# The output product of a graph network: two node blocks in seven block products over halves of columns, the third block plain and last

## The chip, the core and the metric

The kernel runs on one core of one Trainium2 chip. The metric is the device time of one execution in microseconds (us), lower is better. All numbers are 32-bit floats. The engines are TensorE (PE in the profile; PEld is its weight load), VectorE (DVE), ScalarE (ACT), GpSimd (POOL) and SyncE (SP, which here only issues DMA transfers). Each takes its own instructions in order; they wait for each other by semaphores.

## What is computed

The program is an attention layer over a graph of 384 nodes, followed by a relational graph convolution network with two layers. Only the second network is touched. In short:

```python
x = relu(h_text @ w_in + b_in)                     # 384 x 768
for l in range(2):
    h_in = x
    x = rgcn_conv(x, src, dst, edge_type, basis[l], comp[l], root[l], conv_bias[l])
    x = relu(x) + h_in
    x = batchnorm(x, bn_gamma[l], bn_beta[l])      # over the nodes
h_final = x @ w_out + b_out                        # 384x768 by 768x1024
result = residual + layernorm(h_final, ln_gamma, ln_beta)   # over the 1024 columns
```

The product `x @ w_out` and the layer normalisation behind it are the end of the program.

## The kernel before

Features lie on the 128 partitions: after a layer, `XT` is a tile of 128 x 6 x 384, six chunks of 128 features by 384 nodes. Nodes make three blocks of 128. A product accumulates over the six chunks in a PSUM bank of 512 columns. Each matmul of 32-bit floats stands in the trace as two records of PE and two of PEld. Most of the program's products are already made by seven block products instead of eight (Winograd's form): sums of blocks are made beforehand on VectorE, and the products are added up in PSUM banks and on the way out of them.

The order of TensorE, VectorE, ScalarE, GpSimd and SyncE is that of the code (`manual_schedule`); the framework only puts in the waits. So an instruction of VectorE that has to wait holds up everything written after it on VectorE.

The second layer (l = 1) ends as follows. Line numbers are those of the profile.

- The last basis products (L979, L985) make `H_`. The root product (L1019, 72 records) begins the six banks `pr`; inside it `rest()` makes the last block product of the basis stage.
- VectorE makes the sums of the mixed adjacency `At` (T1 to T4, L1082 to L1086) and the first feature sums (L1097).
- `first_of(0)` and the products with `q(1, 0)` follow, and then the loop `for p in range(pairs)` with three passes (products at L1077). A pass makes two chunks of features, o0 = 2p and o1 = 2p + 1, in banks `pa` and `pc`. TensorE's order in a pass is S0·T1 into pc, S1·T2 into pa, S3·q(1,1) into pc, S2·T3 into pa, then the first product of the next pair (into the bank `following`) and h(o1,1)·T4 into pa.
- `take(o, j, ps)` (L1107) adds half a chunk from a bank to `XN` on VectorE. A product that goes on accumulating in a bank waits until the `take` of what was there before has read it: S3·q(1,1) waits for `take(o1, 1, pc)`, S2·T3 for `take(o0, 1, pa)`.
- When a chunk is complete, `rectify` applies ReLU on ScalarE (L1110), `measure` takes the batch statistics (L1042 to L1049), and `normalise_layer` applies them (L1054 to L1058). The last two chunks are XN[4] and XN[5].
- The output product (L1183) reads XN. For each node block t it takes two banks of 512 columns (block 2: one of 512 and two of 256). Block 0 runs over k = 0 to 3 for both banks, and then over k = 4 and 5. VectorE adds the bias (L1187), takes row statistics (L1189), makes mean and deviation (`row_spread`, L156 to L159), applies them (L1194, L1195, L1197), and SP and ACT store the halves.
- The output weights `w_out` come in three parts of two chunks (1 MB each) through SP, in a ring of five buffers `wpool`, which the basis and root weights share.

Storage: `T13` and `T2` (sums of weights) lie in the buffers tagged `hT` and `mask8` of the pool `keep`; `S` (node sums) and `T4` in the pool `cp`. In layer 0 the feature sums borrow two weight buffers of `wpool`, too. `sums` and `rn` are small tiles of the pool `late`, used for the edge counts in layer 0.

Of the kernel before, what the change touches and what calls it, by code (L numbers as in the profile page):

```python
# [10 lines left out]
F32 = mybir.dt.float32  # L11
# [4 lines left out]
ALU = mybir.AluOpType  # L16
# [35 lines left out]
def gnn_kernel(ctx: ExitStack, tc: tile.TileContext, out, x, edges, chunks, cols, rows, small,  # L52
# [36 lines left out]
    def wload(src, shape, name, whole=False):  # L89
        w = wpool.tile([P, *shape], F32, tag="w", name=name)  # L90
        load_rows(w, src, whole)
        return w
# [60 lines left out]
    def row_spread(st):  # L153

        mv = tiny.tile([P, 2], F32, tag="mv", name="mv")
        nc.vector.bn_aggr(mv, st.rearrange("p a b -> p (a b)"))  # L156
        sd = tiny.tile([P, 1], F32, tag="sd", name="sd")
        nc.vector.tensor_scalar(sd, mv[:, 1:2], LN_EPS, None, ALU.add)
        nc.scalar.activation(sd, sd, AF.Sqrt)  # L159
        return mv, sd  # L160
# [190 lines left out]
    taken = []  # L351

    def add_up(r):
        sums[r] = late.tile([P, N], F32, tag="sum", name="sum", bufs=4)
        nc.gpsimd.tensor_tensor(sums[r], A[:, r, 0, :], A[:, r, 1, :], ALU.add)
        nc.gpsimd.tensor_tensor(sums[r], sums[r], A[:, r, 2, :], ALU.add)

    def share(r):

        ps = next_bank("ps_cnt", [i for i in range(8) if i not in taken])  # L360
        nc.tensor.matmul(ps[:, :N], ones, sums[r], start=True, stop=True)
        rn = late.tile([P, N], F32, tag="rn", name="rn", bufs=2)

        nc.scalar.activation(rn, ps[:, :N], AF.Relu, bias=minus)
        nc.scalar.activation(rn, rn, AF.Identity, bias=ones[:, 0:1])
        nc.vector.reciprocal(rn, rn)
        nc.vector.tensor_tensor(A[:, r], A[:, r], rn[:, None, :].to_broadcast([P, NT, N]), ALU.mult)
        if r + 4 < R:
            add_up(r + 4)


    with ExitStack() as inner:
# [261 lines left out]
        soft = soft_stack.enter_context(tc.tile_pool(name="soft", bufs=1, side="right"))  # L634
        At = late.tile([P, B, NT, N], F32, name="At")
        A = late.tile([P, R, NT, N], F32, tag="A", name="A")

        prA = keep.tile([P, KD, N], F32, tag="hT", name="prA")
        prB = soft.tile([P, KD, N], F32, name="prB")
# [266 lines left out]
    with tc.tile_pool(name="conv", bufs=1) as cp:  # L906
# [4 lines left out]
        def block(X, n, i):  # L911

            return X.rearrange("p (c i) n -> p i c n", i=2)[:, i, :, n * P:(n + 1) * P]

        def node_sums(X):
            S = cp.tile([P, 4, 3, P], F32, tag="S", name="S")
            for i, a, b, op in ((0, block(X, 1, 0), block(X, 1, 1), ALU.add), (1, S[:, 0], block(X, 0, 0), ALU.subtract),
                                (2, block(X, 0, 0), block(X, 1, 0), ALU.subtract),
                                (3, block(X, 0, 1), S[:, 1], ALU.subtract)):
                nc.vector.tensor_tensor(S[:, i], a, b, op)  # L920
            return S

        def weight_sums(w):
            T13 = keep.tile([P, 3, 2, HC], F32, tag="hT", name="T13")
            T2 = keep.tile([P, 3, HC], F32, tag="mask8", name="T2")
            for c in range(3):
                nc.vector.tensor_tensor(T13[:, c], w[c][:, :, HC:], w[c][:, 0, :].rearrange("p (o d) -> p o d", o=2),
                                        ALU.subtract)
                nc.vector.tensor_tensor(T2[:, c], w[c][:, 1, HC:], T13[:, c, 0], ALU.subtract)
            return T13[:, :, 0], T2, T13[:, :, 1]  # L930

        def last_sums(w, T2):
            T4 = cp.tile([P, 3, HC], F32, tag="T4", name="T4")
            for c in range(3):
                nc.vector.tensor_tensor(T4[:, c], w[c][:, 1, :HC], T2[:, c], ALU.subtract)
            return T4
# [28 lines left out]
        for l in range(L):  # L965
# [3 lines left out]
            for b in range(B):  # L969
# [6 lines left out]
                def times(ps, x, y, start=False):  # L976

                    for c in range(3):
                        nc.tensor.matmul(ps, x[:, c], y(c), start=start and c == 0, stop=(c == 2),  # L979
                                         skip_group_check=not start)  # L980
# [9 lines left out]
                    go_between(l, b, c)  # L990
                nc.scalar.copy(hs[0][0], pa)  # L991
                nc.vector.tensor_tensor(hs[0][0], hs[0][0], pb, ALU.add)
                times(pc, S[:, 0], lambda c: T[0][:, c], True)
                nc.scalar.copy(hs[2][0], pe)
                nc.scalar.copy(hs[2][1], pf)
                nc.scalar.copy(hs[1][1], pc)
                times(pa, S[:, 1], lambda c: T[1][:, c])
                nc.scalar.copy(hs[0][1], pa)
                times(pc, S[:, 3], lambda c: w[c][:, 1, HC:])
                nc.vector.tensor_tensor(hs[0][1], hs[0][1], pc, ALU.add)  # L1000
                times(pa, S[:, 2], lambda c: T[2][:, c])
                nc.vector.tensor_tensor(hs[1][1], hs[1][1], pa, ALU.add)

                def rest(pa=pa, X=XT, T4=T4, dst=hs[1][0]):
# [12 lines left out]
            for k in range(KC):  # L1017
# [3 lines left out]
                if k == 0:  # L1021
                    rest()
                go_between(l, B, k)
            room2 = keep.tile([P, KD * N], F32, tag="hT", name="room2")
            spaces = [room2[:, 2304:]]
            if l + 1 < L:
                spaces += [v.rearrange("p i k o -> p (i k o)")[:, i * 768:(i + 1) * 768] for v, n in
                           ((cp.tile([P, 4, 3, P], F32, tag="S", name="sums"), 2),
                            (wpool.tile([P, 2, 6, P], F32, tag="w", name="sums"), 2)) for i in range(n)]
                spaces.append(cp.tile([P, 3, HC], F32, tag="T4", name="sums").rearrange("p c d -> p (c d)")[:, :768])  # L1030
                w = load_basis(l + 1, 0)
            else:

                room = late.tile([P, R * NT * N], F32, tag="A", name="room")
                spaces += [room[:, 3 * D + i * 768:3 * D + (i + 1) * 768] for i in range(5)]
                rowsB = room[:, :3 * D].rearrange("p (j d) -> p j d", j=3)
                for j, r in enumerate((R_BOUT, R_LNG, R_LNB)):
                    nc.scalar.dma_start(rowsB[:, j, :], rows[r:r + 1, :].to_broadcast([P, D]))

            def measure(o):  # L1040

# [36 lines left out]
                                     skip_group_check=True)  # L1078

            T1, T2 = [room2[:, i * 1152:(i + 1) * 1152].rearrange("p (c d) -> p c d", c=6) for i in range(2)]  # L1080
            T4 = keep.tile([P, 6, HN], F32, tag="mask8", name="T4")
            nc.vector.tensor_tensor(T1, q(0, 1), q(0, 0), ALU.subtract)  # L1082
            nc.vector.tensor_tensor(T2, q(1, 1), T1, ALU.subtract)
            T3 = q(0, 1)
# [40 lines left out]
            for p in range(pairs):  # L1125
# [34 lines left out]
                take(o1 + 1, 0, following)  # L1160
                ready = measure(rectify(o1))
                pa = following
            XT = XN
            if l + 1 < L:
                S = node_sums(XT)
# [2 lines left out]

        for t in range(NT):
            nc.gpsimd.tensor_tensor(x_sb[:, t, :], x_sb[:, t, :], rowsB[:, 2, :], ALU.add)  # L1170
        w = [wload(w_out[part], (2, D), "w_out") for part in range(3)]
        hf_ = cp.tile([P, NT, D], F32, tag="H", name="hf")
        for t in range(NT):
            hf = hf_[:, t, :]
            last = t == NT - 1
            ps = [next_bank("ps_f") for _ in range(3 if last else 2)]

            parts = [(ps[0], 0, 512), (ps[1][:, :256], 512, 768), (ps[2][:, :256], 768, D)] if last else \
                [(ps[0], 0, 512), (ps[1], 512, D)]
            for ks in ((range(4), range(4, KC)) if t == 0 else (range(KC),)):  # L1180
                for p, c0, c1 in parts:
                    for k in ks:
                        nc.tensor.matmul(p, XT[:, k, t * P:(t + 1) * P], w[k // 2][:, k % 2, c0:c1],  # L1183
                                         start=(k == 0), stop=(k == KC - 1))
            st = tiny.tile([P, 4, 6], F32, tag="st", name="st")
            for p, c0, c1 in parts:
                nc.vector.tensor_tensor(hf[:, c0:c1], p, rowsB[:, 0, c0:c1], ALU.add)  # L1187
                for c in range(c0, c1, 256):
                    nc.vector.bn_stats(st[:, c // 256, :], hf[:, c:c + 256])  # L1189
            mv, sd = row_spread(st)  # L1190

            parts = ((nc.sync, slice(0, 512)), (nc.scalar, slice(512, D)))
            for _, cs in parts:
                nc.vector.scalar_tensor_tensor(hf[:, cs], hf[:, cs], mv[:, 0:1], rowsB[:, 1, cs], ALU.subtract, ALU.mult)  # L1194
            nc.vector.reciprocal(sd, sd)  # L1195
            for queue, cs in parts:
                nc.vector.scalar_tensor_tensor(hf[:, cs], hf[:, cs], sd, x_sb[:, t, cs], ALU.mult, ALU.add)  # L1197
                queue.dma_start(out[t * P:(t + 1) * P, cs], hf[:, cs])


def _by_outputs(w, n):
# [68 lines left out]
```

## Time and profile before

| what | us |
|---|---|
| median of 3 runs | 725.38 (724.61 to 729.79) |
| the profiled execution | 717.47 |
| its span, first to last instruction | 715.7 |
| second layer, TensorE in L1077 | 636.3 to 677.3 |
| output product, TensorE in L1183 | 677.1 to 708.2 |
| from the last matmul to the end | 7.5 |

The page of the profile gives each engine's busy time and the chain of work that ended last. The mean granted clock of TensorE is 0.995 of full speed over the span. Views of the trace give the records in order of time with start and length; "idle before" and an arrow name what ended an engine's wait. Times inside the program are counted from the span's start.

In the stretch from 677.1 to 708.2 us, VectorE is busy for 18.3 us, ScalarE for 1.1. After 708.2 only the normalisation of the third block and the stores of its two halves remain.

### The profile page before, as it was taken

How to read it: one execution, taken by the hardware profiler on the slowest of the kernel's cores; microseconds unless marked ns; L12 is line 12 of the kernel's file. 1: busy time of each engine (PE TensorE's matmuls, PEld its weight loads, DVE VectorE, ACT ScalarE, POOL GpSimd, SP SyncE). 2: the span in 40 equal slices, each digit the busy share in tenths (PEclk: the TensorE clock that was granted, in tenths of full speed). 3: DMA queues.
4: the chain of work that ended last, by engine and by line, in shares of the span. 5: the costliest groups of instructions: out<-in, count | busy, mean ns of one | idle time of the engine just before them, and what ended most of it. 6: DMA issues, size and time to landing. Idle time of an engine off the chain costs nothing.

```text
span 715.7 us, 9149 instructions
## 1 busy us (share of the span) xinstructions
PE 699.9 (98%) x3228; PEld 527.9 (74%) x3228; DVE 512.6 (72%) x1307; ACT 157.6 (22%) x360; POOL 308.1 (43%) x239
## 2 busy tenths in 40 slices
PE   8999999999999999999999999999999999999995
PEld 7759999999997444478985555558975555579943
DVE  5886697868886699787534279798878766507756
ACT  3211111111111577410221124202131111011100
POOL 1366777778687788687786542000000000120000
PEclk9999999999999999999999999999999999999999
DMA  8788787373562622733424994311104322700001
GB/s 303 267 279 264 228 250 212 80 243 67 203 209 43 177 2 1 221 44 45 89 0 103 250 288 153 133 44 45 45 0 133 102 69 94 308 1 1 1 30 59
DMA packets 69180, 91.04 MB, mean 127 GB/s; under 512 B 22940, under 2 KB 50688, under 8 KB 68750
## 3 DMA queue, kind: packets, MB, share of 16 engines
q1 hardware_dynamic: 46830, 78.45, 32.6%
q0 software_dynamic: 21296, 9.60, 10.8%
q10 hardware_dynamic: 1008, 2.41, 0.9%
q8 instruction: 25, 0.41, 0.2%
q14 instruction: 21, 0.17, 0.1%
HBM read 79.27 MB, written 11.16 MB: 126 GB/s over the span
## 4 chain that ended last, share of the span: by engine, by line
PE 87%; DVE 10%; ACT 2%; DMA 1%; issue 0%; DVEq 0%; ACTq 0%
PE ps_g L985 12%; PE ps_g L979 10%; PE ps_k L402 10%; PE ps_c L1077 10%; PE ps_v L402 8%; PE ps_q L420 6%; PE ps_q L402 5%; PE ps_f L1183 4%; DVE At L348 4%; PE ps_y L402 3%; PE ps_c L1019 3%; PE ps_x L402 3%; PE ps_o L707 2%; PE ps_s L662 2%; PE ps_pT L696 2%; PE ps_v L586 2%
## 5 line engine op out<-in xcount | busy, mean ns | idle before, releaser
L283 POOL DMA_INDIRECT atab<-count,at x99 | 166.3, 1679 | 44.2 <-issue 23.5
L278 POOL DMA_INDIRECT mtab<-m_val,at x99 | 103.4, 1045 | 57.6 <-issue 22.9
L1170 POOL TENSOR_TENSOR x_sb<-x_sb,room 128x1024 f32<-128x1024 f32 x3 | 7.0, 2348 | 188.9 <-DMA room<-in_rows 188.9
L348 DVE SCALAR_TENSOR_TENSOR At<-A,small_sb,At 128x1152 f32<-128x1152 f32 x40 | 53.6, 1414 | 0.0
L979 PE MATMUL ps_g<-T,S 128*128 128x384 f32 x144 | 49.1, 486 | 0.0
L985 PE MATMUL ps_g<-w_c,XN 128*128 128x384 f32 x144 | 47.7, 487 | 1.1 <-DVE XN L1107 1.1
L985 PE MATMUL ps_g<-w_c,XT 128*128 128x384 f32 x144 | 47.9, 486 | 0.0
L420 PE MATMUL ps_q<-hT,w_q 128*128 128x384 f32 (+1 forms) x160 | 43.4, 435 | 1.4 <-DVE hT L108 1.4
L985 PEld LDWEIGHTS ps_g<-w_c,XN 128*128 128x128 f32 x144 | 27.3, 190 | 20.2 <-DVE XN L1107 1.4
L979 PEld LDWEIGHTS ps_g<-T,S 128*128 128x128 f32 x144 | 27.3, 190 | 19.2 <-ACT H L991 0.4
L985 PEld LDWEIGHTS ps_g<-w_c,XT 128*128 128x128 f32 x144 | 27.3, 190 | 18.8
L420 PEld LDWEIGHTS ps_q<-hT,w_q 128*128 128x128 f32 x160 | 30.1, 200 | 14.1 <-ACT hT L101 1.7
L1077 PE MATMUL ps_c<-At,H 128*128 128x192 f32 x216 | 36.4, 326 | 0.0
L1077 PEld LDWEIGHTS ps_c<-At,H 128*128 128x128 f32 x216 | 35.4, 190 | 0.5
L402 PE MATMUL ps_k<-T,S 128*128 128x192 f32 x192 | 35.1, 326 | 0.0
L1107 DVE TENSOR_TENSOR XN<-XN,ps_c 128x192 f32<-128x192 f32 x38 | 12.5, 349 | 30.8 <-ACT XN L1063 19.7
L402 PEld LDWEIGHTS ps_k<-T,S 128*128 128x128 f32 x192 | 31.8, 190 | 0.0
L1183 PE MATMUL ps_f<-w_out,XN 128*128 128x512 f32 (+1 forms) x84 | 31.1, 531 | 0.0
L675 DVE CUSTOM_DVE_ANT_0 s<-ps_s,mask 128x384 f32<-128x384 f32 x48 | 24.5, 550 | 5.3 <-PE ps_s L662 5.3
L267 DVE SCALAR_TENSOR_TENSOR same<-cells,own,later 128x128 f32<-128x128 int32 x99 | 28.0, 350 | 0.4
L267 DVE SCALAR_TENSOR_TENSOR same<-keys,key,weigh 128x128 f32<-128x128 int32 x99 | 27.9, 349 | 0.0
L1183 PEld LDWEIGHTS ps_f<-w_out,XN 128*128 128x128 f32 x84 | 15.9, 190 | 14.9 <-issue 14.3
(298 smaller groups left out, 1411.6 us busy)
## 6 DMA issues: line engine op xcount, KB each, us to landing
w_c<-in_basis SPq DMA_DIRECT2D x96, 192.0 KB, 4.1
atab<-zero SPq DMA_DIRECT2D x36, 192.0 KB, 5.2
A<-atab POOLq DMA_DIRECT2D x12, 576.0 KB, 9.0
keys<-keys_d SPq DMA_DIRECT2D x25, 192.0 KB, 5.1
w_c<-in_root SPq DMA_DIRECT2D x6, 768.0 KB, 7.1
w_q<-in_wiq SPq DMA_DIRECT2D x16, 256.0 KB, 6.4
w_k<-in_wk SPq DMA_DIRECT2D x16, 256.0 KB, 5.8
w_k<-in_wik SPq DMA_DIRECT2D x16, 256.0 KB, 3.0
```

Source lines behind the costliest of these rows:

```text
L267: nc.vector.scalar_tensor_tensor(same, row[:, n, :], mine[:, c:c + 1], times, ALU.is_equal, ALU.mult, accum_out=count[:, i, c:c + 1])
L278: nc.gpsimd.indirect_dma_start(mtab[c // PER][:, :], bass.IndirectOffsetOnAxis(at[:, 0, c:c + 1], 0), m_val[:, c:c + 1], None)
L283: nc.gpsimd.indirect_dma_start(atab[0 if i < 11 else i % 2][:, :], bass.IndirectOffsetOnAxis(at[:, 1, c:c + 1], 0), count[:, 1, c:c + 1], ...
L348: nc.vector.scalar_tensor_tensor(At[:, b], A[:, r], w, At[:, b], ALU.mult, ALU.add)
L402: nc.tensor.matmul(ps, a[:, k, :], b[:, k, :], start=start and k == 0, stop=(k == 3), skip_group_check=not start)
L420: nc.tensor.matmul(ps[o][:, c], wt_[:, k, o * P:(o + 1) * P], src[:, k, c], start=(k == 0 and c.start == 0), stop=(k == KD - 1 and c.stop ...
L675: nc.vector.tensor_tensor_reduce(s[j], ps[:, :N], mask8[:, t, :], -scale, 3.0e38, ALU.add, ALU.min, tops[:, j:j + 1])
L979: nc.tensor.matmul(ps, x[:, c], y(c), start=start and c == 0, stop=(c == 2), skip_group_check=not start)
L985: nc.tensor.matmul(ps, block(XT, n, i)[:, c], w[c][:, i, o * HC:(o + 1) * HC], start=(first and c == 0), stop=(c == 2 and (i == 1 or ps is ...
L1019: nc.tensor.matmul(pr[o], w[k // 2][:, k % 2, o * P:(o + 1) * P], XT[:, k, :], start=(k == 0), stop=(k == KC - 1))
L1077: nc.tensor.matmul(ps, x[:, c], y[:, c], start=start and c == 0, stop=stop and c == 5, skip_group_check=True)
L1183: nc.tensor.matmul(p, XT[:, k, t * P:(t + 1) * P], w[k // 2][:, k % 2, c0:c1], start=(k == 0), stop=(k == KC - 1))
```

## The change

The output product of node blocks 0 and 1 is made in seven block products over halves: halves of the features (even and odd chunks), two node blocks, and halves of the 1024 columns. Each of the seven has three matmuls of 512 columns. Block 2 stays plain and is made last. The sums of weights (`out_sums`, twelve subtractions of 128 x 512) are made on VectorE in three places: four before the adjacency sums of the last layer, four at the end of the first pass of the pairs, four at the end of the second. The sums of nodes (`OS`, four of 128 x 384) are made after the last normalisation. `w_end` is the load of the output weights, written ahead of the loop. Storage is put together so that room for these sums is found: `x_all`, `room2`, `mroom` and `sum_room` each take the place of several tiles.

```diff
     def add_up(r):
-        sums[r] = late.tile([P, N], F32, tag="sum", name="sum", bufs=4)
+        sums[r] = sum_room[:, r % 4]
...
-        rn = late.tile([P, N], F32, tag="rn", name="rn", bufs=2)
+        rn = sum_room[:, 4 + r % 2]
...
+        sum_room = late.tile([P, 6, N], F32, name="sum_room")
...
+        x_all = cp.tile([P, 4 * 3 * N], F32, name="x_all")
+        x_room = [x_all[:, i * 3 * N:(i + 1) * 3 * N] for i in range(4)]
+        room2 = keep.tile([P, KD * N], F32, tag="hT", name="room2")
+        mroom = keep.tile([P, 6, HN], F32, tag="mask8", name="mroom")
...
             spaces = [room2[:, 2304:]]
             if l + 1 < L:
-                spaces += [v.rearrange("p i k o -> p (i k o)")[:, i * 768:(i + 1) * 768] for v, n in
-                           ((cp.tile([P, 4, 3, P], F32, tag="S", name="sums"), 2),
-                            (wpool.tile([P, 2, 6, P], F32, tag="w", name="sums"), 2)) for i in range(n)]
-                spaces.append(cp.tile([P, 3, HC], F32, tag="T4", name="sums").rearrange("p c d -> p (c d)")[:, :768])
+                spaces += [x_all[:, i * 768:(i + 1) * 768] for i in range(5)]
                 w = load_basis(l + 1, 0)
             else:
...
+                w_end = [wload(w_out[part], (2, D), "w_out") for part in range(3)]
+                out_T = [v.rearrange("p (c o) -> p c o", c=3) for v in
+                         [x_all[:, i * 1536:(i + 1) * 1536] for i in range(3)]
+                         + [sum_room.rearrange("p r n -> p (r n)")[:, :1536]]]
+                def out_sums(*which):
+                    for i, c in which:
+                        x, y = [(b_end(0, 1), b_end(0, 0)), (b_end(1, 1), lambda c: out_T[0][:, c]),
+                                (b_end(1, 1), b_end(0, 1)), (b_end(1, 0), lambda c: out_T[1][:, c])][i]
+                        nc.vector.tensor_tensor(out_T[i][:, c], x(c), y(c), ALU.subtract)
+                def b_end(i, half):
+                    return lambda c: w_end[c][:, i, half * 512:(half + 1) * 512]
+                out_sums((0, 0), (1, 0), (0, 1), (1, 1))
...
                 ready = measure(rectify(o1))
                 pa = following
+                if l + 1 == L:
+                    out_sums(*(((2, 0), (3, 0), (2, 1), (3, 1)) if p == 0 else ((0, 2), (1, 2), (2, 2), (3, 2))))
...
-        w = [wload(w_out[part], (2, D), "w_out") for part in range(3)]
...
+        for dst, x, y, op in ((OS[0], block(XT, 1, 0), block(XT, 1, 1), ALU.add),
+                              (OS[1], OS[0], block(XT, 0, 0), ALU.subtract),
+                              (OS[2], block(XT, 0, 0), block(XT, 1, 0), ALU.subtract),
+                              (OS[3], block(XT, 0, 1), OS[1], ALU.subtract)):
+            nc.vector.tensor_tensor(dst, x, y, op)
+        def put_out(t, c0, ps, first, done):
+            cs = slice(c0, c0 + ps.shape[1])
+            nc.vector.tensor_tensor(hf_[:, t, cs], ps, rowsB[:, 0, cs] if first else hf_[:, t, cs], ALU.add)
+            for c in range(c0, cs.stop, 256) if done else ():
+                nc.vector.bn_stats(st[t][:, c // 256, :], hf_[:, t, c:c + 256])
...
+        def times(ps, x, y, start=False):
+            for c in range(3):
+                nc.tensor.matmul(ps, x[:, c], y(c), start=start and c == 0, stop=(c == 2), skip_group_check=not start)
...
+        pa, pb, pc, pd = [next_bank("ps_f") for _ in range(4)]
+        times(pa, block(XT, 0, 0), b_end(0, 0), True)
+        put_out(0, 0, pa, True, False)
+        times(pb, block(XT, 0, 1), b_end(1, 0), True)
+        put_out(0, 0, pb, False, True)
+        times(pc, OS[0], summed(0), True)
+        put_out(1, 512, pc, True, False)
+        times(pa, OS[1], summed(1))
+        put_out(0, 512, pa, True, False)
+        times(pc, OS[3], b_end(1, 1))
+        put_out(0, 512, pc, False, True)
+        times(pd, block(XT, 1, 1), summed(3), True)
+        put_out(1, 0, pd, True, False)
+        times(pa, OS[2], summed(2))
+        finish(0)
+        put_out(1, 0, pa, False, True)
+        put_out(1, 512, pa, False, True)
...
+        for p, c0 in parts:
+            for k in range(KC):
+                nc.tensor.matmul(p, XT[:, k, 2 * P:], w_end[k // 2][:, k % 2, c0:c0 + p.shape[1]],
+                                 start=(k == 0), stop=(k == KC - 1))
+        finish(1)
+        for p, c0 in parts:
+            put_out(2, c0, p, True, True)
+        finish(2)
```

`block(X, n, i)` is node block n with the even (i = 0) or odd (i = 1) chunks; `summed(i)` is `out_T[i]`; `finish(t)` is the normalisation and the stores of block t as before (`row_spread`, L1194 to L1198). `node_sums`, `weight_sums` and `last_sums` only get their storage from the new tiles.

More of the change, by code (lines that the diff above doesn't have):

```diff
@@ L913, in block @@
             return X.rearrange("p (c i) n -> p i c n", i=2)[:, i, :, n * P:(n + 1) * P]
+        x_all = cp.tile([P, 4 * 3 * N], F32, name="x_all")
+        x_room = [x_all[:, i * 3 * N:(i + 1) * 3 * N] for i in range(4)]
+        room2 = keep.tile([P, KD * N], F32, tag="hT", name="room2")
+        mroom = keep.tile([P, 6, HN], F32, tag="mask8", name="mroom")
         def node_sums(X):
[L916 to L920, printed above, removed]
+            S = [v.rearrange("p (c n) -> p c n", c=3) for v in
+                 [x_room[0][:, i * N:(i + 1) * N] for i in range(3)] + [x_room[1][:, :N]]]
+            for dst, a, b, op in ((S[0], block(X, 1, 0), block(X, 1, 1), ALU.add), (S[1], S[0], block(X, 0, 0), ALU.subtract),
+                                  (S[2], block(X, 0, 0), block(X, 1, 0), ALU.subtract),
+                                  (S[3], block(X, 0, 1), S[1], ALU.subtract)):
+                nc.vector.tensor_tensor(dst, a, b, op)
             return S
         def weight_sums(w):
-            T13 = keep.tile([P, 3, 2, HC], F32, tag="hT", name="T13")
-            T2 = keep.tile([P, 3, HC], F32, tag="mask8", name="T2")
+            T13 = room2[:, :6 * HC].rearrange("p (c o d) -> p c o d", c=3, o=2)
+            T2 = mroom.rearrange("p c n -> p (c n)").rearrange("p (c d) -> p c d", c=3)
             for c in range(3):
@@ L932, in last_sums @@
         def last_sums(w, T2):
-            T4 = cp.tile([P, 3, HC], F32, tag="T4", name="T4")
+            T4 = x_room[2].rearrange("p (c d) -> p c d", c=3)
             for c in range(3):
@@ L992, in gnn_kernel @@
                 nc.vector.tensor_tensor(hs[0][0], hs[0][0], pb, ALU.add)
-                times(pc, S[:, 0], lambda c: T[0][:, c], True)
+                times(pc, S[0], lambda c: T[0][:, c], True)
                 nc.scalar.copy(hs[2][0], pe)
@@ L996, in gnn_kernel @@
                 nc.scalar.copy(hs[1][1], pc)
-                times(pa, S[:, 1], lambda c: T[1][:, c])
+                times(pa, S[1], lambda c: T[1][:, c])
                 nc.scalar.copy(hs[0][1], pa)
-                times(pc, S[:, 3], lambda c: w[c][:, 1, HC:])
+                times(pc, S[3], lambda c: w[c][:, 1, HC:])
                 nc.vector.tensor_tensor(hs[0][1], hs[0][1], pc, ALU.add)
-                times(pa, S[:, 2], lambda c: T[2][:, c])
+                times(pa, S[2], lambda c: T[2][:, c])
                 nc.vector.tensor_tensor(hs[1][1], hs[1][1], pa, ALU.add)
@@ L1023, in gnn_kernel @@
                 go_between(l, B, k)
-            room2 = keep.tile([P, KD * N], F32, tag="hT", name="room2")
             spaces = [room2[:, 2304:]]
             if l + 1 < L:
-                spaces += [v.rearrange("p i k o -> p (i k o)")[:, i * 768:(i + 1) * 768] for v, n in
-                           ((cp.tile([P, 4, 3, P], F32, tag="S", name="sums"), 2),
-                            (wpool.tile([P, 2, 6, P], F32, tag="w", name="sums"), 2)) for i in range(n)]
-                spaces.append(cp.tile([P, 3, HC], F32, tag="T4", name="sums").rearrange("p c d -> p (c d)")[:, :768])
+                spaces += [x_all[:, i * 768:(i + 1) * 768] for i in range(5)]
                 w = load_basis(l + 1, 0)
@@ L1080, in gnn_kernel @@
             T1, T2 = [room2[:, i * 1152:(i + 1) * 1152].rearrange("p (c d) -> p c d", c=6) for i in range(2)]
-            T4 = keep.tile([P, 6, HN], F32, tag="mask8", name="T4")
+            T4 = mroom
             nc.vector.tensor_tensor(T1, q(0, 1), q(0, 0), ALU.subtract)
@@ L1170, in gnn_kernel, with finish @@
             nc.gpsimd.tensor_tensor(x_sb[:, t, :], x_sb[:, t, :], rowsB[:, 2, :], ALU.add)
-        w = [wload(w_out[part], (2, D), "w_out") for part in range(3)]
         hf_ = cp.tile([P, NT, D], F32, tag="H", name="hf")
-        for t in range(NT):
-            hf = hf_[:, t, :]
[L1175 to L1190, printed above, removed]
+        OS = [mroom.rearrange("p c n -> p (c n)")[:, i * N:(i + 1) * N] for i in range(3)] + [room2[:, :N]]
+        OS = [v.rearrange("p (c n) -> p c n", c=3) for v in OS]
+        for dst, x, y, op in ((OS[0], block(XT, 1, 0), block(XT, 1, 1), ALU.add),
[3 more added lines that the diff above has]
+            nc.vector.tensor_tensor(dst, x, y, op)
+        st = [tiny.tile([P, 4, 6], F32, tag="st", name="st") for _ in range(NT)]
+        def put_out(t, c0, ps, first, done):
[3 more added lines that the diff above has]
+                nc.vector.bn_stats(st[t][:, c // 256, :], hf_[:, t, c:c + 256])
+        def finish(t):
+            hf = hf_[:, t, :]
+            mv, sd = row_spread(st[t])
             parts = ((nc.sync, slice(0, 512)), (nc.scalar, slice(512, D)))
@@ L1198, in gnn_kernel, with summed @@
                 queue.dma_start(out[t * P:(t + 1) * P, cs], hf[:, cs])
+        def times(ps, x, y, start=False):
+            for c in range(3):
+                nc.tensor.matmul(ps, x[:, c], y(c), start=start and c == 0, stop=(c == 2), skip_group_check=not start)
+        def summed(i):
+            return lambda c: out_T[i][:, c]
+        pa, pb, pc, pd = [next_bank("ps_f") for _ in range(4)]
[15 more added lines that the diff above has]
+        put_out(1, 512, pa, False, True)
+        ps = [next_bank("ps_f") for _ in range(3)]
+        parts = [(ps[0], 0), (ps[1][:, :256], 512), (ps[2][:, :256], 768)]
+        for p, c0 in parts:
[6 more added lines that the diff above has]
+        finish(2)
 def _by_outputs(w, n):
```

## The prediction

> **What bounds the kernel now.** I read the busy shares first, then the chain of waits near the end, then the timelines of TensorE and VectorE there, because the change acts only there. The busy line and two rows of the chain (start, length, what):
>
> ```profile
> PE 699.9 (98%) x3228; PEld 527.9 (74%) x3228; DVE 512.6 (72%) x1307; ACT 157.6 (22%) x360; POOL 308.1 (43%) x239
> ...
> 636.34 40.95 PE ps_c L1077 x252
> 677.29 30.94 PE ps_f L1183 x84
> ```
>
> TensorE is the bound: from 636.34 to 708.2 us it does nothing but the products of the second layer (L1077) and the output product (L1183), without a gap; then VectorE finishes the last node block and 7.5 us pass to the end (715.7). Work taken from L1183 is therefore worth its full streaming time, and any wait put into L1077 costs its full length. What the stage consists of, and its weights:
>
> ```profile
> L1183 PE MATMUL ps_f<-w_out,XN x84: 379/592/593, 677.1 to 707.8; 128*128 128x512 f32 x60, 128*128 128x256 f32 x24
> L87 SPq DMA_DIRECT2D w_out<-in_w_out x3: 328/328/328, 608.6 to 620.9; - x3
> DMA to landing us min/median/max: 7.8/7.8/7.8
> ```
>
> Each matmul of the code is two records, so these are 30 of 512 columns and 12 of 256. 60 x 512 + 24 x 256 = 36,864 columns in 31.1 us are 0.844 ns a column, 0.864 us for one matmul of 512 columns. The weights have landed by 620.9 + 7.8 = 628.7. Last, where TensorE and VectorE hand over in the last two of the three passes of the loop over pairs (TensorE, then VectorE):
>
> ```profile
> 659.58 2.12 PE L1077 MATMUL ps_c<-At,room 128*128 128x192 f32 x12
> 661.52 4.07 PE L1077 MATMUL ps_c<-At,H 128*128 128x192 f32 x24
> ...
> 671.27 2.11 PE L1077 MATMUL ps_c<-At,room 128*128 128x192 f32 x12
> ...
> 677.12 31.09 PE L1183 MATMUL ps_f<-w_out,XN 128*128 128x512 f32 x84
> ```
>
> ```profile
> 658.29 0.15 DVE L1048 TENSOR_SCALAR sc<-mvb 128x1 f32<-128x1 f32 x1
> 658.36 0.34 DVE L1107 TENSOR_TENSOR XN<-XN,ps_c 128x192 f32<-128x192 f32 x1
> ...
> 665.89 0.95 DVE L1097 TENSOR_TENSOR H<-H 128x768 f32<-128x768 f32 x1
> 666.76 0.95 DVE L1097 TENSOR_TENSOR room<-H,room 128x768 f32<-128x768 f32 x1
> 667.63 0.61 DVE L1107 TENSOR_TENSOR XN<-XN,ps_c 128x192 f32<-128x192 f32 x2
> 668.63 0.56 DVE L1042 TENSOR_TENSOR XN<-XN 128x384 f32<-128x384 f32 x1 [0.39 <-ACT XN L1110]
> ...
> 670.03 0.15 DVE L1048 TENSOR_SCALAR sc<-mvb 128x1 f32<-128x1 f32 x1
> 670.11 0.34 DVE L1107 TENSOR_TENSOR XN<-XN,ps_c 128x192 f32<-128x192 f32 x1
> ...
> 681.57 0.48 DVE L1058 TENSOR_SCALAR XN<-XN,sc 128x384 f32<-128x384 f32 x1
> 685.91 0.69 DVE L1187 TENSOR_TENSOR hf<-ps_f,room 128x512 f32<-128x512 f32 x1 [3.85 <-PE ps_f L1183]
> ```
>
> The matmuls at 659.58 and 671.27 are the products S3·q(1,1). They add into the bank pc that `take(o1, 1, pc)` must have read; that read is the L1107 at 658.36 (ends 658.70) and at 670.11 (ends 670.45). So the slack is 0.88 and 0.82 us: VectorE is 72% busy on average, but here it is nearly in step with TensorE.
>
> **Removed.** Blocks 0 and 1 took 24 matmuls of 512 columns; seven products of three take 21. Three fewer are 3 x 0.864 = 2.6 us, all on the path.
>
> **Added within the pairs: `out_sums` on VectorE.** After `measure(rectify(o1))` of passes 0 and 1 stand four subtractions of 128x512, and the next `take(o1, 1, pc)` is queued behind them. Width: 768 elements last 0.95 and 384 last 0.56, so 512 last 0.69. Independent ones start 0.08 before the one ahead ends (665.89, 666.76, 667.63: 0.87 apart), so 0.61 apart; pass 1 has a dependent pair (0.72). Pass 0 inserts 4 x 0.61 = 2.45 us, pass 1 0.72 + 3 x 0.61 = 2.56. The Trainium skill, "VectorE: DVE Perf Modes", section Terms, has a flush after every op, the next not issuing until the pipe is empty; by that they would be 4 x 0.69 = 2.76 each, 0.5 more together. The row decides: overlap is seen.
>
> Now step by step. Pass 1: take moves from 658.36 to 660.81, ends 661.15; S3 starts at 661.2 instead of 659.58 and ends at 663.25 (a restart costs 0.1: twelve matmuls after the stall at 495.17 took 2.22 instead of 2.11). S2·T3 waits for `take(o0, 1, pa)`, moved by 2.45 to end at 663.56: TensorE starts it at 663.6, 2.1 late. VectorE keeps its 2.45, since between here and pass 2 its waits are for ScalarE's ReLU (L1042), which follow it. Pass 2: `take` at 670.11 + 2.45 + 2.56 = 675.12, ends 675.46; S3 starts at 675.5 instead of 671.27, with its restart 4.3 us late. Equally: 5.0 inserted, less 0.8 slack, plus handover. From there on TensorE leads, and everything, the last normalised block XN[5] (682.05, now 686.4) included, is 4.3 late.
>
> **Output stage.** It starts at 681.4. Formerly eight matmuls (k 0 to 3) came before any needing XN[4] or XN[5]; now pa wants k 0, 2, 4 and pb wants k 1, 3, 5. XN[4] is in time (677.52 + 4.3 = 681.8, wanted at 683.1). XN[5] is wanted after five matmuls, 681.4 + 4.3 = 685.75, and comes at 686.4: 0.65 of stall, 0.1 of restart. The four node sums follow on VectorE (0.56 each): the first ends at 686.9, wanted at 687.4; OS[1] ends about 687.5, wanted at 690; hidden behind pb and pc. Reuse of pa and pc: their first reads (`put_out`, 0.69) queue behind the node sums and end at about 689.1 and 691.3, wanted at 690.0 and 692.6: no stall.
>
> **The tail.** VectorE gets four more additions from PSUM (0.72 with its start) and those sums, 5 us, over a stage that left it idle for 12.8 of 31.1 us (18.3 busy between 677.1 and 708.2); what matters is the order. After pd's product (697.8 by this count) it must do put_out of pd 0.72, finish(0) 3.4 (689.14 to 692.5 today), two put_outs with statistics 1.47 each, finish(1) 3.4, and block 2's first two parts 1.47 + 0.87: ready at 710.6. TensorE ends at 681.4 + 28.5 + 0.75 = 710.7 (33,792 columns x 0.844 = 28.5). A near tie: I add 0.1; late finishing work would next show here, between 0 and 0.6 (if an operation overlapped as little as by the flush rule). The last 7.5 us, block 2 alone, are unchanged.
>
> **Costed at nothing.** The first four `out_sums` stand before L1082 and wait for the second weight part. Loads were issued from 608.63, the second 0.65 later, so VectorE, ready at 611.8, waits until 616.4 and for `rest()` on TensorE until 616.9; it finishes at 619.2, and the weight sums and first feature sums (5.4 + 3.7 us) at 628.3. They are wanted at 643.98: 15.7 us of cover; without it each us would count. SP: the root loads, then the output weights, then stores, the same order as before; the trace already shows these loads run ahead, so there is no queue to be passed. ACT: the three row loads keep their place. POOL: the three residual additions (624.2 to 631.2) are unchanged; VectorE's shifted sums now end beside them, and should that slow them, the 15.7 us cover it. `sum_room`, `x_all`, `room2` and `mroom` rename storage: the waits of the built program stay alike but for layer 0, where two sums no longer occupy weight buffers and SP's 19.4 us wait for L1097 goes. No TensorE wait of the trace is for a weight of layer 1, so 0 (bounds -0.5 to 0).
>
> **Sum.** -2.6 + 4.3 + 0.75 + 0.1 = +2.6 us: span 715.7 to 718.3, the profiled execution 717.47 to 720.0. The median shown, 725.38, is 7.9 above that execution; I put the same difference on it: 728.0, +0.35%.
>
> **Rivals.** *Cover where I see none*: if the inserted subtractions found room (slack larger than the two rows say), only -2.6 + 0.75 stays: 723.5. For it: VectorE idles 28% overall. Against: both slacks are under 0.9 and the insertions are 2.5. Chance 0.14.
>
> *The clock (the slower side)*: the waits come to about 1.6 and 0.5 us in pass 1 and 2.2 in pass 2. The Trainium skill, "TensorE: Matmul & The Clock Gate", section "Part 1: The HAM clock gate", says an idle window of about 3.4 us halves the clock until a busy window has passed. The row: after the 1.07 us wait at 526.6, matmuls last 486 ns as elsewhere and the granted clock stays 1.00. If each of the two waits tripped it, 3.4 us of work would take 6.8 twice: 2.6 + 6.8 = 9.4, 734.8. It decides from an idle stretch near 3.4 us; mine are below. Chance 0.06.
>
> *The change is not what it says*: the built program has 27 matmuls of 512 columns instead of 30, in the order described; chance 0.02 for something that leaves the time at 725.4. What is left, 0.78, is my sum with its sizes.
>
> **From cases to numbers.** Own range of the sum: restart and overlap move it from +1.5 to +3.7; three runs span 724.61 to 729.79, so a median moves by some 2 us: 725 to 731. The rival with cover widens the range down to 722.5; 731.5 leaves out the clock. About 1% (7.3 us) is what a measurement of this kernel tells from no change. Faster by that: no case gets there (the whole gain is 2.6 us), 0.03 for scatter. Slower: the clock 0.06 and unseen delays 0.04, 0.10. Same: 0.87.
>
> **What would show it.** Right: L1183's successors hold 78 records and about 28.5 us; TensorE waits for VectorE before S3 of pass 1 and pass 2 (about 1.6 and 2 us), and once more (about 0.7) at the sixth matmul of the output stage; the output stage starts near 681.4. Wrong: no such waits (cover); a granted clock under 1.00 after them; a VectorE wait for the output weights that reaches past 640; or an end more than 7.7 us behind the last matmul (the tail).

## The result, and the profile after

The changed kernel takes 732.28 us (median of 20 runs) where the kernel before takes 727.65 beside it; the ratio of the two is 1.0039, 95% interval 1.0015 to 1.0064. The medians take in all runs; the ratio compares the fast ones alone, because some runs fell into a slower state. That is 0.4% slower, 2.8 us of 727.65 (between 1.1 and 4.7): a small slowing that the interval sets apart from none. 0.35% had been forecast.

The profiled execution of the changed kernel is 734.78 us with a span of 733.0, 17.3 longer than the one before. Most of that is not the change: at the first root product of the second layer it is already 13.2 us later (624.22 against 611.02). Between 50 and 250 us, where the code is the same, TensorE is idle for 10.3 us in this execution and not in the other; in two later profiles of the same changed kernel it is busy there without a gap, too (200.00 of 200.00 us). All comparisons of traces below therefore use the **late stage**: from the first matmul of the second layer's root product to the end of the span. It is 715.7 - 611.02 = 104.7 us before and 733.0 - 624.22 = 108.8 after. The two marks (before, changed):

```profile
611.02 4.03 PE L1019 MATMUL ps_c<-XN,w_c 128*128 128x384 f32 x12
```

```profile
624.22 4.03 PE L1026 MATMUL ps_c<-XN,w_c 128*128 128x384 f32 x12
```

The busy shares of the changed kernel:

```profile
PE 703.0 (96%) x3222; PEld 528.2 (72%) x3222; DVE 533.6 (73%) x1327; ACT 157.1 (21%) x360; POOL 311.6 (43%) x239
```

Six records of TensorE are gone (the three matmuls), twenty of VectorE are new. The timeline of TensorE in the changed kernel, from the second pass of the pairs on (start, length, what; in brackets the idle time before and what ended it):

```profile
674.36 2.22 PE L1096 MATMUL ps_c<-At,room 128*128 128x192 f32 x12 [1.43 <-DVE XN L1126]
676.66 4.17 PE L1096 MATMUL ps_c<-At,H 128*128 128x192 f32 x24
...
688.53 3.90 PE L1096 MATMUL ps_c<-At,room 128*128 128x192 f32 x12 [1.86 <-DVE XN L1126]
692.27 2.11 PE L1096 MATMUL ps_c<-mroom,H 128*128 128x192 f32 x12
...
696.17 4.46 PE L1224 MATMUL ps_f<-w_out,XN 128*128 128x512 f32 x10
701.15 1.12 PE L1224 MATMUL ps_f<-w_out,XN 128*128 128x512 f32 x2 [0.53 <-DVE XN L1077]
...
714.99 10.49 PE L1250 MATMUL ps_f<-w_out,XN 128*128 128x512 f32 x36
```

Before, TensorE had no gap here. Now it waits 1.43 us before S3·q(1,1) of pass 1 (674.36), 1.86 before that of pass 2 (688.53), and 0.53 in the output stage before the sixth matmul, the one that needs XN[5]. VectorE shows who is late (the same kernel, timeline of VectorE):

```profile
671.48 0.15 DVE L1067 TENSOR_SCALAR sc<-mvb 128x1 f32<-128x1 f32 x1
671.55 0.68 DVE L1052 TENSOR_TENSOR x_all<-w_out 128x512 f32<-128x512 f32 x1
672.15 0.68 DVE L1052 TENSOR_TENSOR sum_room<-w_out,x_all 128x512 f32<-128x512 f32 x1
672.75 0.69 DVE L1052 TENSOR_TENSOR x_all<-w_out 128x512 f32<-128x512 f32 x1
673.36 0.68 DVE L1052 TENSOR_TENSOR sum_room<-w_out,x_all 128x512 f32<-128x512 f32 x1
673.96 0.35 DVE L1126 TENSOR_TENSOR XN<-XN,ps_c 128x192 f32<-128x192 f32 x1
```

Four subtractions (L1052) start 0.60 us apart; the `take` (L1126) comes behind them at 673.96, and the matmul follows 0.05 us after its end.

One thing in the first view is no wait. The twelve matmuls at 688.53 last 3.90 us; the same twelve at 674.36 last 2.22. The view by windows says why (length; busy time and records of PE, PEld, DVE, ACT, POOL; granted clock; DMA share and GB/s):

```profile
685.43:688.84 3.41, 1.55 (x10) 1.26 (x9) 3.27 (x10) 0.20 (x1) 0.00 (x0) 1.00 0.00 0
688.84:692.25 3.41, 3.41 (x12) 3.41 (x11) 1.00 (x4) 0.00 (x0) 0.00 (x0) 0.50 0.01 2
692.25:695.67 3.42, 3.42 (x22) 3.42 (x22) 2.13 (x7) 0.73 (x2) 0.00 (x0) 1.00 0.02 5
```

Behind the wait the granted clock is 0.50 for 3.41 us. In that time TensorE gets through 12 records; in the next, at full clock, through 22. The twelve matmuls alone take 3.90 - 2.22 = 1.7 us longer, in this execution.

### The profile page after: what moved, and what is told of

Its sections match the earlier page's. It is cut to its first block, busy times and chain, and to the rows that moved or that the text cites. A ratio compares the mean times of both kernels' runs of the same rounds, so it can differ in the third digit from the quotient of the medians.

```text
span 733.0 us, 9169 instructions
## 1 busy us (share of the span) xinstructions
PE 703.0 (96%) x3222; PEld 528.2 (72%) x3222; DVE 533.6 (73%) x1327; ACT 157.1 (21%) x360; POOL 311.6 (43%) x239
## 4 chain that ended last, share of the span: by engine, by line
PE 80%; DVE 12%; ACT 2%; issue 2%; another core or an unknown queue 1%; DMA 1%; SPq 1%; DVEq 0%; ACTq 0%
PE ps_g L992 12%; PE ps_g L986 10%; PE ps_k L402 9%; PE ps_v L402 7%; PE ps_c L1096 6%; PE ps_q L420 6%; PE ps_q L402 4%; DVE At L348 4%; PE ps_y L402 3%; PE ps_x L402 3%; PE ps_c L1026 3%; PE ps_s L663 3%; PE ps_o L708 3%; PE ps_pT L697 2%; PE ps_v L586 2%
## 5 line engine op out<-in xcount | busy, mean ns | idle before, releaser
L1191 POOL TENSOR_TENSOR x_sb<-x_sb,room 128x1024 f32<-128x1024 f32 x3 | 9.0, 3035 | 190.8 <-DVE mroom L1105 190.8
L986 PE MATMUL ps_g<-room,x_all 128*128 128x384 f32 x96 | 33.6, 486 | 0.0
L1007 DVE TENSOR_TENSOR H<-H,ps_g 128x384 f32<-128x384 f32 x8 | 4.4, 553 | 32.9 <-PE ps_g L986 32.9
L986 PEld LDWEIGHTS ps_g<-room,x_all 128*128 128x128 f32 x96 | 18.2, 190 | 12.7
L1126 DVE TENSOR_TENSOR XN<-XN,ps_c 128x192 f32<-128x192 f32 x38 | 12.5, 349 | 19.4 <-PE ps_c L1096 12.2
L934 DVE TENSOR_TENSOR room<-w_c 128x768 f32<-128x768 f32 x24 | 23.3, 973 | 2.9 <-DMA w_c<-in_basis 2.9
```

## The experiments

Late stages of all profiles but those of the two ladders further down, from the same two marks (span minus the start of the first root matmul):

| kernel | late stage, us | against before |
|---|---|---|
| before | 715.7 - 611.02 = 104.7 | |
| changed | 733.0 - 624.22 = 108.8 | +4.1, with one stretch at half clock |
| changed, again | 716.8 - 609.68 = 107.1 | +2.4, clock full |
| changed, timed | 718.4 - 611.35 = 107.0 | +2.4, clock full |
| all sums before the loop | 724.1 - 621.15 = 102.9 | -1.7 |
| pass 0's sums before the loop | 738.4 - 633.60 = 104.8 | +0.1 |
| the sums without the products | 740.3 - 629.76 = 110.5 | +5.9, one stretch at half clock |
| sums before the loop, four matmuls ahead | 727.1 - 622.28 = 104.8 | +0.1 |
| sums before the loop, one matmul ahead | 711.6 - 609.46 = 102.1 | -2.5 |

**All eight loop sums moved ahead of the loop.**

```diff
             for _ in feature_sums(0):
                 pass
+            if l + 1 == L:
+                out_sums((2, 0), (3, 0), (2, 1), (3, 1), (0, 2), (1, 2), (2, 2), (3, 2))
...
-                if l + 1 == L:
-                    out_sums(*(((2, 0), (3, 0), (2, 1), (3, 1)) if p == 0 else ((0, 2), (1, 2), (2, 2), (3, 2))))
```

> The changed kernel with the eight subtractions of the two loop passes moved ahead of the loop over pairs, behind the first feature sums; the seven products stay. I call late stage the time from the first matmul of the second layer's root product to the end of the span: 104.7 us in the kernel before, 108.8 in the changed one. Theory (waits): no wait of TensorE before S3 in passes 1 and 2, no lowered clock, only the wait of about 0.65 us in the output stage; late stage 104.7 - 2.6 + 0.75 = 102.9 us, and the whole time 0.25% under the kernel before. Rival (load): what costs is VectorE's added work as such, above all the additions and node sums of the output stage; then moving eight subtractions changes little, the late stage stays at 107 us or more. Rival (port): the eight subtractions now lie beside GpSimd's residual additions, and if both slow each other as the feature sums did in the changed kernel (3.1 us for 0.95), the loop starts late and the late stage is over 104.

Measured: ratio to the kernel before 0.9961, interval 0.9933 to 0.9989; late stage 102.9. Both waits before S3 are gone, the clock stays at 1.00, and only the wait in the output stage is left:

```profile
692.24 1.12 PE L1224 MATMUL ps_f<-w_out,XN 128*128 128x512 f32 x2 [0.52 <-DVE XN L1077]
```

The waits theory holds to 0.1 us and the load rival falls: VectorE does exactly the same work as in the changed kernel, and the late stage is shorter than in the kernel before. The port rival had a point that cost nothing. This is VectorE, and the GpSimd additions beside it, in this kernel:

```profile
633.98 0.95 DVE L1116 TENSOR_TENSOR room<-H 128x768 f32<-128x768 f32 x1
634.97 2.99 DVE L1116 TENSOR_TENSOR room<-room,H 128x768 f32<-128x768 f32 x1
637.88 3.11 DVE L1116 TENSOR_TENSOR H<-H 128x768 f32<-128x768 f32 x1
640.91 3.10 DVE L1116 TENSOR_TENSOR room<-H,room 128x768 f32<-128x768 f32 x1
643.93 0.68 DVE L1052 TENSOR_TENSOR x_all<-w_out 128x512 f32<-128x512 f32 x1
...
651.02 0.35 DVE L1128 TENSOR_TENSOR XN<-XN,ps_c 128x192 f32<-128x192 f32 x1 [2.07 <-ACT XN L1082]
```

```profile
634.11 9.09 POOL L1191 TENSOR_TENSOR x_sb<-x_sb,room 128x1024 f32<-128x1024 f32 x3 [195.12 <-DVE mroom L1105]
```

While GpSimd adds (634.11 to 643.2), the same VectorE operation takes 3.1 us instead of 0.95. But the eight moved subtractions run behind it, at 0.68 each, and VectorE still waits 2.07 us for ScalarE before its first `take` at 651.02. In the kernel before, the wait at this place was 19.66 us:

```profile
640.89 0.35 DVE L1107 TENSOR_TENSOR XN<-XN,ps_c 128x192 f32<-128x192 f32 x1 [19.66 <-ACT XN L1063]
```

**Only pass 0's sums moved.** The diff is the last one with only the first four sums ahead of the loop; the line in the loop stays for p == 1, with the other four.

> As the last, but only the four subtractions of pass 0 are moved ahead; those of pass 1 stay. Waits: no wait in pass 1; before S3 of pass 2 TensorE waits 2.56 - 0.82 = 1.7 us and a handover, 1.8; late stage 102.9 + 1.8 + 0.1 = 104.8 us if the clock stays, 106.5 if it falls as in the changed kernel, where it was 0.50 for about 3.3 us behind an idle 2.0 us and cost 1.75 us. Load: 107 or more as before.

Measured: late stage 104.8. TensorE, and the windows that hold the wait and what follows it:

```profile
695.61 2.22 PE L1096 MATMUL ps_c<-At,room 128*128 128x192 f32 x12 [1.59 <-DVE XN L1128]
```

```profile
693.90:695.60 1.70, 0.12 (x1) 0.00 (x0) 1.70 (x5) 0.00 (x0) 0.00 (x0) 1.00 0.00 0
695.60:699.00 3.40, 3.39 (x21) 3.39 (x22) 1.73 (x8) 0.52 (x1) 0.00 (x0) 1.00 0.01 2
```

A wait of 1.59 us, the twelve matmuls at 2.22, the clock full: four sums in one place cost 104.8 - 102.9 = 1.9 us.

**The sums without the seven products.** The end of the kernel before stands behind the changed loop; the sums are made and not used:

```diff
-        pa, pb, pc, pd = [next_bank("ps_f") for _ in range(4)]
...
+        w = w_end
+        for t in range(NT):
...
+                        nc.tensor.matmul(p, XT[:, k, t * P:(t + 1) * P], w[k // 2][:, k % 2, c0:c1],
+                                         start=(k == 0), stop=(k == KC - 1))
```

> One part alone: storage, early load and all twelve subtractions as in the changed kernel, but the output product is the plain one of the kernel before (the sums are made and not used). Waits: the waits before S3 as in the changed kernel; late stage 104.7 + 4.3 = 109.0 us, and 1.75 more if the clock falls. Load: near 104.7, since the output stage has none of the added work.

Measured: late stage 110.5. The waits are those of the changed kernel (1.43 us in pass 1 and the one below), the clock falls as in its first profile, and the output product is as before:

```profile
694.08 3.90 PE L1096 MATMUL ps_c<-At,room 128*128 128x192 f32 x12 [1.85 <-DVE XN L1126]
...
701.71 31.09 PE L1204 MATMUL ps_f<-w_out,XN 128*128 128x512 f32 x84
```

So the cost lies in the loop; without the products nothing of it comes back. Of the 5.9 us, 1.7 belong to the clock; the 4.2 that are left come near the 4.3 that the prediction has for the loop.

**Filling the wait of the output stage, with four matmuls and with one.**

```diff
+        def plain(p, c0, ks):
+            for k in ks:
+                nc.tensor.matmul(p, XT[:, k, 2 * P:], w_end[k // 2][:, k % 2, c0:c0 + p.shape[1]],
+                                 start=(k == 0), stop=(k == KC - 1))
...
+        plain(p0, 0, range(4))
         times(pa, block(XT, 0, 0), b_end(0, 0), True)
```

The third block then makes only the rest of those columns at its own place. The second version has `range(1)` there, and `finish(0)` moved up, ahead of `put_out(1, 0, pd, True, False)`.

> The first experiment, and four matmuls of the third block (k 0 to 3 of its first 512 columns) are made first in the output stage, so that XN[5] is wanted after nine matmuls (7.8 us) instead of five. Waits: no wait in the output stage, late stage 102.9 - 0.75 = 102.1 us, 2.6 under the kernel before, whole time 0.36% under it. Load: no better than the first experiment. A tail bound by VectorE would show as more than 7.6 us from the last matmul to the end.

Measured with four: ratio 0.998, interval 0.9944 to 1.0016, so no difference that was shown; late stage 104.8, where 102.1 was expected, and worse than the 102.9 without the filling. No wait of TensorE was left, but its last matmul ends at 716.9, and VectorE's last PSUM reads are at:

```profile
718.90 0.41 DVE L1205 TENSOR_TENSOR hf<-ps_f,room 128x256 f32<-128x256 f32 x1
719.34 0.43 DVE L1207 BATCH_NORM_STATS2 st<-hf 128x6 f32<-128x256 f32 x1
719.69 0.41 DVE L1205 TENSOR_TENSOR hf<-ps_f,room 128x256 f32<-128x256 f32 x1
```

There is no bracket: VectorE waits for nothing, it is itself late with the row work of blocks 0 and 1. Four matmuls ahead of these blocks put that work off: `finish(0)` starts 85.8 us after the first root matmul (708.07 - 622.28) instead of 83.2 (704.31 - 621.15 without the filling), and fewer matmuls are left behind it. Matmuls taken from the end of the stage had been its cover.

> The first experiment (sums before the loop), with one matmul of the third block made first in the output stage instead of four, and finish(0) written ahead of the put_out of pd. Reason: with four, the late stage did not fall (104.8 us), because the last matmul came 3.5 us sooner and VectorE's row work did not. Waits and tail: no wait of TensorE in the output stage, the last matmul 28.5 us after the first, VectorE ready within 0.2 us of it; late stage 102.9 - 0.6 = 102.3 us, whole time 0.34% under the kernel before. If instead the first experiment's wait was no cost, or VectorE's tail is bound by more than order, the late stage is 102.9 or more.

Measured with one: ratio 0.9964, interval 0.995 to 0.9978; late stage 102.1. The same read now waits for TensorE:

```profile
704.12 0.42 DVE L1205 TENSOR_TENSOR hf<-ps_f,room 128x256 f32<-128x256 f32 x1 [0.61 <-PE ps_f L1232]
```

The late stage is 2.5 us shorter than before, nearly all of the 2.6 that three matmuls are worth. The median is 713.5 us (6 runs) where the kernel before has 716.14 beside it: 0.4% faster than before, where the changed kernel was 0.4% slower. Two things were changed at once here; what the earlier `finish(0)` gives alone was not measured.

**The clock: the changed kernel again, and two ladders of waits.** The ladders are the kernel with the sums before the loop, with dummy subtractions in pass 1 (four in layer 0 and six in layer 1; then five and eight):

```diff
+                if p == 1:
+                    flat = sum_room.rearrange("p r n -> p (r n)")
+                    for i in range((4, 6)[l]):
+                        nc.vector.tensor_tensor(dummy[:, i % 2], flat[:, :512], flat[:, 512:1024], ALU.subtract)
```

> The changed kernel once more. Its waits are fixed by order: 1.4 us before S3 of pass 1, 1.9 before S3 of pass 2, 0.5 in the output stage. Theory (half a stretch): the granted clock is set for stretches of 3.41 us that run freely; it falls for the next one when TensorE idles over half of one. 1.4 is never enough, 1.9 is when it lies inside one stretch, which is about half of the executions; so the late stage is 107.1 us or 108.8, by the clock alone. Rival (fixed): the fall belongs to this wait and comes each time, 108.8.

Measured: late stage 107.1. The same wait, and the clock stays (with the marks that are used at the end):

```profile
609.68 4.03 PE L1026 MATMUL ps_c<-XN,w_c 128*128 128x384 f32 x12
...
674.00 2.22 PE L1096 MATMUL ps_c<-At,room 128*128 128x192 f32 x12 [1.85 <-DVE XN L1126]
...
679.95 4.46 PE L1224 MATMUL ps_f<-w_out,XN 128*128 128x512 f32 x10
...
698.76 10.49 PE L1250 MATMUL ps_f<-w_out,XN 128*128 128x512 f32 x36
```

> To the first experiment, dummy subtractions of 128x512 are added on VectorE before the same take in pass 1 of the loop (so that S3 of pass 2 waits): four in the first layer, six in the second; nothing else changes. Waits: 4 x 0.61 - 0.8 = 1.65 us and 6 x 0.61 - 0.8 = 2.85. Half a stretch: the clock stays after the first and falls after the second in most executions (it must hold 1.71 us of idle in one stretch). Whole window: the clock stays after both, since neither idles for 3.4 us. Late stage 102.95 + 2.85 = 105.8 us, and 1.7 more if the clock falls there.

> As ladder a with five dummy subtractions in the first layer and eight in the second: waits of 2.25 and 4.1 us. Half a stretch: the first falls in about three of four executions, the second always. Whole window: the first never; the second not always. Late stage 102.95 + 4.1 = 107.05 us, and 1.7 more for each stretch at half clock.

Ladder a, then ladder b, TensorE:

```profile
522.50 2.22 PE L1097 MATMUL ps_c<-At,x_all 128*128 128x192 f32 x12 [1.47 <-DVE XN L1129]
...
676.10 2.22 PE L1097 MATMUL ps_c<-At,room 128*128 128x192 f32 x12 [2.68 <-DVE XN L1129]
```

```profile
521.31 3.00 PE L1097 MATMUL ps_c<-At,x_all 128*128 128x192 f32 x12 [2.07 <-DVE XN L1129]
...
677.42 4.21 PE L1097 MATMUL ps_c<-At,room 128*128 128x192 f32 x12 [3.88 <-DVE XN L1129]
```

Late stages: 718.9 - 613.00 = 105.9 us and 722.6 - 613.12 = 109.5, the second with its clock halved behind S3. Lengths of 2.22 are full clock, longer ones are not. Waits of 1.47 and 2.68 us left the clock alone; waits of 2.07, 3.88 and, in two of four profiles, 1.86 did not. So the length of the wait alone doesn't decide, and that a fall needs a whole stretch of 3.4 us idle is refuted by 2.07 and 1.86.

Where the wait lies does bear on it. The trace records the clock in stretches of 3.41 us (or whole multiples). Laid over these, the wait of 1.86 falls into one stretch in the two profiles where the clock fell; in the two where it stayed it is split, 0.89 + 0.97 us (the changed kernel again) and 1.26 + 0.60 (the changed kernel, timed). Ladder a's 2.68 us are split, too, 1.82 + 0.86; TensorE is busy for 1.60 us of the first stretch and 2.55 of the second:

```profile
671.82:675.24 3.42, 1.60 (x10) 1.30 (x9) 3.38 (x8) 0.20 (x1) 0.00 (x0) 1.00 0.00 0
675.24:678.65 3.41, 2.55 (x16) 2.55 (x17) 2.40 (x9) 0.00 (x0) 0.00 (x0) 1.00 0.00 0
```

In all eleven profiles, from the first record of the clock to the last matmul, 13 stretches at full clock have 1.85 us or more of idle time in them, and behind 12 of them the clock is 0.50. Behind every stretch at full clock with 1.82 us or less it stays. The limit of "half a stretch", 1.71 us, that was expected is therefore too low: stretches with 1.74, 1.76, 1.80 and 1.82 us (the last in ladder a) were not followed by a fall. One exception is open: a stretch with 1.99 us, at 202.5 us in the kernel with all sums before the loop, was not followed by one.

> The changed kernel, timed, to see how often the clock falls. The three profiles with this order of waits (the changed kernel twice, and the one with the sums alone) have 1.85 us idle before S3 of pass 2; the clock fell in two of the three. Half a stretch: the idle has to lie inside one stretch of 3.41 us to be over half of it, so in about (3.41 - 1.86) / 3.41 = 45% of the executions, or a little more, the time is 1.7 us longer; on a quiet chip the executions stand in two groups, 2.4 and 4.1 us above the kernel before, which itself makes one group. Rival (fixed): one group, at 2.4 or at 4.1.

Measured: ratio 1.0042, interval 1.0023 to 1.0061. The ten times are 718.16 to 718.45 (four), 719.68 to 720.15 (four) and 722.75, 722.78. The kernel before was expected to make one group; it made three: 715.94 to 716.13 (nine), 717.66 to 717.75 (three), 719.00 to 719.22 (three). Steps of about 1.7 us are in both kernels, and the run of 720.15, which was profiled, has its half-clock stretch at 13 us, in the start of the program, with the clock full behind S3. So the lowest groups compare cleanly, 718.3 against 716.0: 2.3 us. How often the clock falls at S3 can't be counted from these times.

## Why the prediction was right

The sum was +2.6 us, made of four terms. A profile with a full clock behind S3 measures each (the changed kernel again: output stage from 679.95, its last matmul to 709.25, span 716.8):

- *The waits in the loop, +4.3.* From the root product to the output stage it is 679.95 - 609.68 = 70.27 us against 677.12 - 611.02 = 66.10: +4.17. The slack of 0.88 and 0.82 us, the width of a 128x512 subtraction (0.69 said, 0.68 measured) and the distance between them (0.61 said, 0.60 measured) were read off the right rows. The overlap in these rows was right, too, against the flush after each operation that the prediction set beside it, which would have put them 0.69 apart.
- *Three matmuls less, -2.6, and the wait for XN[5], +0.75.* The output stage lasts 709.25 - 679.95 = 29.30 us, against 31.09: -1.79, where -1.85 was said. The wait was 0.52 with 0.1 of restart, a little shorter than the 0.75.
- *The tail, +0.1.* From the last matmul to the end it is 7.55 us against 7.49. VectorE was nearer to being late than before, though not as near as the 0.1 us that the prediction worked out: ahead of its last read it still waits 0.60 us for TensorE (the row below the list), where it was 1.70 in the kernel before. The version with four matmuls ahead took away the cover and lost 1.9 us by it.
- *Costed at nothing.* The four early sums waited 2.91 us for the first weight part and 1.06 for the second, where one wait of 4.6 (611.8 to 616.4) was worked out, and were hidden. The first feature sums ended at 647.0 in the changed kernel's first profile, 5.5 us later than worked out (628.3 and the 13.2 of that execution's offset), as three of them ran into GpSimd's additions; the 15.7 us of cover took it. The loads of layer 1 brought nothing: in the changed kernel, timed, the root product begins at 611.35, before at 611.02, both with one half-clock stretch at the start.

```profile
709.30 0.42 DVE L1205 TENSOR_TENSOR hf<-ps_f,room 128x256 f32<-128x256 f32 x1 [0.60 <-PE ps_f L1250]
```

Together 4.17 - 1.79 + 0.06 = +2.44 us with the clock full. The measured ratio, 2.8 us, lies between this and the 4.1 of the execution whose clock fell. Its interval, 1.1 to 4.7, holds both, so that 0.35% and 0.39% come so close is in part luck; what bears the prediction out is its terms. As a bare time, 732.28 lies above the 722.5 to 731.5 that was given: that range stood on three runs with a median of 725.38, and in twenty the same kernel has 727.65.

The point that the prediction had wrong is the rival of the clock. It said of the clock, "It decides from an idle stretch near 3.4 us; mine are below", and gave it 0.06. A wait of 1.86 us was enough in two of four profiles, so a sign that it had named as wrong, a granted clock under 1.00 behind a wait, did appear. The price per fall was set too high: it took 3.4 us of work to last 6.8, a loss of 3.4, but the half clock lasts 3.41 us in all and costs 1.7. And it fell behind one of the two waits only, never behind the 1.43 us of pass 1, so the rival's 734.8 does not come about: with one fall the changed kernel is 4.1 us behind, not 9.4. That the number held although the clock falls is luck: the loss is small, and whether it comes depends on where the wait lies in the clock's stretches. Of the other rivals, cover that wasn't seen did not exist, and the change does what it says.

## What to carry to other kernels

Before putting work on an engine that is "72% busy", read how late each of its handovers already is: here twice 2.5 us of subtractions met one slack of 0.8 us, while 20 us of idle time of the same engine lay one stage earlier. Work saved at the end of a stage can be the cover of what another engine still has to do; take it from where that engine waits, not from where it is late. A wait of TensorE may cost more than its length, and whether it does can change from execution to execution, so compare stages of traces with the granted clock beside them.

## What was not expected of the hardware

- A wait of TensorE of 1.86 us, inside one of the clock's stretches of 3.41 us, was followed by a halved clock in the next (granted 0.50), which cost another 1.7 us; a longer one (2.68 us) that was split over two stretches, 1.82 and 0.86, left the clock full.
- VectorE's additions and subtractions of two tensors, 0.95 us alone for 128x768, take 3.0 to 3.1 us while GpSimd adds two tensors; GpSimd's own 128x1024 additions go from 2.35 us, in the kernel before, where VectorE is idle beside them, to 3.03 (9.09 for three).
